# A macaron layer with 4-bit weights: order and engines of the unpacking in the first stage

## The chip, the core and the metric

The kernel runs on one core of a Trainium2 chip. Its time is that of the device, in microseconds (us); the number given is a median over runs. The profile's engines are TensorE (PE: matmuls; PEld: its weight loads), VectorE (DVE), ScalarE (ACT), GpSimd (POOL) and SyncE (SP), which mostly issues transfers (DMAs). A name with a q (SPq) is an engine's queue.

## The reference

Two half-weighted gated feed-forward blocks stand around a convolution, each behind a layer norm and added to its input. The feed-forward weights are 4-bit numbers, eight to an int32 word, with a zero point and a scale for each group of 128 input rows.

```python
def _dequant(qweight, scales, qzeros, g_idx):          # shifts = 4 * (0 .. 7)
    w = (qw[:, None, :] >> shifts[None, :, None] & MAXQ).reshape(-1, qweight.shape[1])
    z = ((qz[:, :, None] >> shifts[None, None, :] & MAXQ) + 1).reshape(qzeros.shape[0], -1)
    return (w.astype(scales.dtype) - z[g_idx].astype(scales.dtype)) * scales[g_idx]

def _L0_ffn_ref(x, ...):
    h = _silu(xf @ Wg) * (xf @ Wu)                     # HID 1024, INTER 2752, groups of 128 rows
    return (h @ Wd).reshape(...)

def _L0_attn_ref(u, ...):                              # S4: a long convolution along each row
    y = jnp.fft.irfft(jnp.fft.rfft(u, n=n) * jnp.fft.rfft(K, n=n), n=n)[..., :L]
    return y + D[0] * u

x = L0_attn_u                                          # (2, 1024, 1024) float32
x = x + 0.5 * _L0_ffn_ref(_layernorm(x), ...)
x = x + _L0_attn_ref(_layernorm(x), ...)
x = x + 0.5 * _L0_ffn_ref(_layernorm(x), ...)
```

## The kernel before, in words

**Jobs and steps.** The 2048 rows of x are taken in four batches of 512, each through two feed-forward blocks: eight jobs, with the convolution between two blocks hung beside the steps of other jobs. A job has a gate/up stage of 64 steps and a down stage of 44. The 43 units of 128 gate or up columns go in eight waves: five of six units, two of four, one of five (lines 38 and 39); a wave has eight steps, one for each group of 128 input rows. In a step each unit gets two matmuls, for the high part (xTh, rounded float32) and the low part (xTl, float16) of the input (line 689). Then ACT or DVE multiplies the unit's PSUM bank in place by a ratio of two groups' scales (lines 659 and 661); here this is called an eviction. The unit's next matmul waits for it. After a wave's last step g, hf, hh and hl are made (lines 714 to 724).

**Unpacking, once.** Only the first job unpacks. For each wave, words (fetch) and spread zero points (fetch_zeros) are loaded; DVE splits the words into two arrays of signed bytes in six operations (signed_bytes: two shifts with masks, two additions, two XORs); POOL copies out eight strided byte planes (dequantize), and each is stored by SP in a DRAM scratch, wq. Every job then loads byte tiles of 128 rows from wq four steps ahead of use (load_bytes, line 621) and POOL, or in the first job at some steps ACT, casts them to float32 three steps ahead (make_weights, lines 635 and 637). Waves 1 to 7 are unpacked beside the steps of the wave before, as first_weights lays down; the down weights follow in the same manner. POOL also makes hh and hl.

**Opening.** start runs ahead of step 0. Wave 0 is split by first_split; ACT makes the four even planes and POOL the four odd ones. Of each plane SP sends sixteen rows directly into the first byte tile (line 496) and the whole to wq (line 497). Meanwhile the moments of the first four row tiles are taken (ACT for tiles 1 and 3, DVE for 0 and 2), the rows are normalized (first_rows) and turned by PE transposes (first_turn), with a copy on ACT (xTh) and a subtraction on DVE (xTl) for each of eight chunks. Chunks 0 and 1 are in start, 2 to 7 at steps 0 to 5, chunk g is used from step g on. keep_warm issues transposes without use on PE. zero_points makes the table of zero points in DRAM, from which fetch_zeros reads; scales turns scale rows into the ratios.

**What sets the order.** at(up, s, f) hangs f on step s; it is written before that step's matmuls. The framework then orders each engine's instructions by its own reckoning, except where in_order_of_writing chains those of named engines. Each engine, and SP with its DMA queue, goes through its list in order and stops at the first entry that must wait. Buffers come from rings: ten of 4 KB a partition (t4: x, words, zeros, even, long scale rows), four for byte planes (qpool), six byte tiles, five weight tiles.

In before, a wave's schedule is this, with s0 = 8w - 12 for w above 2:

```python
at(up, s0 - 3, lambda both=both: in_order_of_writing(both, ET.SP))   # word and zero loads
in_pieces(at, [(up, s0 - 1)], lambda w=w: split(w))                  # six DVE operations, one step
s = s0 + j if w > 2 else j // 2 + s0 * (w - 1)                       # eight copies and stores
```

Of the kernel before, what the change touches and what calls it, by code (L numbers as in the profile page):

```python
# [55 lines left out]
def macaron_s4_kernel(  # L56
# [250 lines left out]
    def zero_points(which, z):  # L307

        p, n = z.shape
        zi, tab = (t2(f"{a}_{which}").bitcast(I32)[:p, : 8 * n] for a in ("zi", "ztab"))  # L310
        unpacked_zeros(tab, z, zi)
        dst, seg, queue = (zd_dram, SEGD, nc.sync) if which else (z_dram, SEG, nc.scalar)
        queue.dma_start(dst.rearrange("g (s n) -> (g s) n", s=seg), tab)

    def inverse(inv, s, name):

# [5 lines left out]
    def scale_rows(k0, k1, queue=nc.sync):  # L322
        n = k1 - k0
        row = t4(f"srow_{k0}") if n > 4 else t2(f"srow_{k0}")
        for m, src in enumerate((gate_s, up_s)):
            queue.dma_start(row[m * GK : (m + 1) * GK, : n * P], src[:, k0 * P : k1 * P])
        return row

    def scales(k0, k1, row):


        n = k1 - k0
        ps = bank(f"ps_s{k0}")
        u0, u1 = 2 * k0, 2 * k1
        for k in range(n):
            nc.tensor.transpose(
                ps[:, bass.ts(k, 2 * GK)], row[: 2 * GK, bass.ts(k, P)], ident[: 2 * GK, : 2 * GK]
            )
        if k1 == WIDE:
            row = t2("srow_half")  # L340
            for m, src in enumerate((gate_s, up_s)):
                nc.sync.dma_start(row[:GK, m * HALF : (m + 1) * HALF], src[:, WIDE * P :])
            nc.tensor.transpose(ps[:, bass.ts(2 * n, GK)], row[:GK, :P], ident[:GK, :GK])
# [131 lines left out]
    def first_split(zq):  # L475


        n = width_of(0)
        z, zi, even = (t4(f"{a}_w0").bitcast(I32)[:, :n] for a in ("z", "zi", "even"))
        raw = packed.pop(0)[0]  # L480
        unpacked_zeros(z, zq, zi)
        nc.vector.tensor_scalar(even, raw, 3, NIBBLES, ALU.logical_shift_left, ALU.bitwise_and)
        nc.vector.tensor_scalar(raw, raw, 1, NIBBLES, ALU.logical_shift_right, ALU.bitwise_and)
        for part in (even, raw):
            both = part.bitcast(U16)
            nc.vector.tensor_tensor(both, both, z.bitcast(U16), ALU.add)
        nc.vector.tensor_scalar(both, both, 0x8080, None, ALU.bitwise_xor)

        def dequantize(j):
            q = qpool.tile([P, n], I8, tag="q", name=f"q_0_{j}")  # L490
            view = lambda a, dt: a.bitcast(dt).rearrange("p (n k) -> p k n", k=4)[:, j // 2, :]
            if j % 2:
                nc.gpsimd.tensor_copy(q, view(raw, I8))
            else:
                nc.scalar.activation(q, view(even, U8), AF.Identity, bias=minus_128)
            nc.sync.dma_start(first_tile[j:P:8], q[: P // 8])
            nc.sync.dma_start(w_q[0].rearrange("(r j) n -> j r n", j=8)[j], q)

        return dequantize

    def signed_bytes(key, raw, even, z):

        nc.vector.tensor_scalar(even, raw, 3, NIBBLES, ALU.logical_shift_left, ALU.bitwise_and)
        yield
        nc.vector.tensor_scalar(raw, raw, 1, NIBBLES, ALU.logical_shift_right, ALU.bitwise_and)
        yield
        for part in (even, raw):
            both = part.bitcast(U16)  # L510
            nc.vector.tensor_tensor(both, both, z.bitcast(U16), ALU.add)  # L511
            yield
            nc.vector.tensor_scalar(both, both, 0x8080, None, ALU.bitwise_xor)
            yield
        view = lambda a: a.bitcast(I8).rearrange("p (n k) -> p k n", k=4)
        packed[key] = view(even), view(raw)

    def split(w):
        raw, z = packed[w]
# [59 lines left out]
    def first_weights(up, dn, at):  # L579


        for w in range(1, len(WAVES)):
            s0 = 8 * w - 12 if w != 2 else 7
            if w > 1:
                both = lambda w=w: (fetch(w), fetch_zeros(w))
                at(up, s0 - 3, lambda both=both: in_order_of_writing(both, ET.SP))
                in_pieces(at, [(up, s0 - 1)], lambda w=w: split(w))
            else:
                both = lambda: [None for _ in split(1)]
                at(up, 0, lambda both=both: in_order_of_writing(both, *STARTING))  # L590
            for j in range(8):
                s = s0 + j if w > 2 else j // 2 + s0 * (w - 1)
                at(up, s, lambda w=w, j=j: dequantize(w, j))
        s0 = len(STEPS) - 12
        when = lambda n: (up, s0 + n) if n < 12 else (dn, (5 * (n - 12)) // 6)
        for n in range(6 * 8):
            k, j = divmod(n, 8)
            a, rt = divmod(k, 3)
            if j == 0:
                at(*when(max(0, n - 7)), lambda a=a, rt=rt: fetch_down(a, rt))  # L600
                steps = [when(max(0, n - d)) for d in (4, 3, 3, 2, 1, 0)]
                in_pieces(at, steps, lambda a=a, rt=rt: split_down(a, rt))
            at(*when(n), lambda a=a, rt=rt, j=j: dequantize_down(a, rt, j))
# [743 lines left out]
    def fast():  # L1347
        for j, (b, k) in enumerate(JOBS):
# [49 lines left out]
                    at(up, 4, store)  # L1398
            if j == 0:
                rows = {3: srow_next}  # L1400
                for s, k0, k1 in ((4, 3, 9), (16, 9, 15), (32, 15, WIDE)):
                    if k0 > 3:
                        load = lambda k0=k0, k1=k1: rows.update({k0: scale_rows(k0, k1)})
                        at(up, s - 5, load)
                    at(up, s - 2, lambda k0=k0, k1=k1: scales(k0, k1, rows.pop(k0)))
                at(up, 40, scales_down)
                zeros = lambda: zero_points(1, zeros_down)
                at(up, 12, lambda: in_order_of_writing(zeros, ET.DVE, ET.SP))
                for c in range(2, NC):
# [46 lines left out]
    STARTING = ET.Activation, ET.DVE, ET.SP  # L1456
    first = {}

    def first_moments():
# [32 lines left out]
    def first_turn(c):  # L1492
# [20 lines left out]
    def keep_warm(n, src=None):  # L1513
# [5 lines left out]
    def start():  # L1519
# [32 lines left out]
        return rows_next, zeros_down  # L1552

    srow_next, zeros_down = in_order_of_writing(start, *STARTING, ET.PE)
# [88 lines left out]
```

## Time and profile before

| | |
|---|---|
| median of 3 runs | 2140.01 us (2137.66 to 2141.07) |
| profiled execution: its time, its span | 2140.35 us, 2138.6 us |
| first gate/up matmul | 21.75 us |
| end of the first job's gate/up stage | about 204 us |
| first gate/up matmul of the second job | about 300 us |
| PE busy in 0 to 20, 20 to 40, 60 to 80 us | 6.07, 15.26, 15.94 us |
| PE busy in 100 to 160 us | 60.00 us |
| granted PE clock over the whole span | 0.995 |

Times within the profile count from the span's start. A matmul's end is modelled, so PE can be shown busy without being at its peak; the number of matmuls in a window says more. Engines other than PE may idle without cost as long as PE is fed.

### The profile page before, as it was taken

The numbers are of one execution on the slowest core, as the hardware profiler recorded it, in microseconds if no ns is written. First come the engines' busy times: TensorE is split into PE (matmuls) and PEld (weight loads), VectorE is DVE, ScalarE is ACT, GpSimd is POOL, SyncE is SP. The second block draws the span as 40 slices with busy tenths as digits, with TensorE's granted clock in tenths as the row PEclk, the third lists the DMA queues.
The fourth block names the chain that finished last, engine by engine and source line by source line (L and its number), as shares of the span: only waits on it lengthen the run. The fifth ranks groups of instructions, "written<-read, shape, count | busy, mean of one in ns | idle before, by whom it ended". The sixth has DMA issues, their size and how long they took to land.

```text
span 2138.6 us, 30244 instructions
## 1 busy us (share of the span) xinstructions
PE 2089.9 (98%) x9744; PEld 1426.0 (67%) x9744; DVE 1700.3 (80%) x2785; ACT 1420.2 (66%) x2233; POOL 1055.2 (49%) x1424
## 2 busy tenths in 40 slices
PE   6899999999999999999999999999999999999998
PEld 4455675677776578665876568675686766866576
DVE  8888877779888777778777888878788787777776
ACT  6787777746655776676766766547776467767765
POOL 3767848653354543546335543454534545345642
PEclk9999999999999999999999999999999999999999
DMA  4335322112111211212121121112111121121111
GB/s 140 108 87 149 91 81 55 35 55 78 43 38 54 91 51 44 74 32 93 54 81 38 30 72 38 36 52 78 35 37 38 52 97 45 45 81 35 33 35 58
DMA packets 163686, 132.14 MB, mean 62 GB/s; under 512 B 22651, under 2 KB 151172, under 8 KB 163518
## 3 DMA queue, kind: packets, MB, share of 16 engines
q1 hardware_dynamic: 162646, 128.65, 19.8%
q8 instruction: 79, 1.29, 0.3%
q10 hardware_dynamic: 872, 1.47, 0.2%
q14 instruction: 89, 0.73, 0.1%
HBM read 104.45 MB, written 25.50 MB: 61 GB/s over the span
## 4 chain that ended last, share of the span: by engine, by line
PE 89%; DVE 6%; POOL 2%; DMA 1%; issue 1%; ACT 1%; SPq 0%; ACTq 0%; DVEq 0%; POOLq 0%
PE pg L689 54%; PE po L752 27%; PE pc L1078 3%; PE pb L774 1%; DVE pg L661 1%; PE pb L1078 1%; PE pt L228 1%; DVE po L661 1%; PE st L228 1%; DMA wq<-q 0%; DMA z<-z_dram 0%; DVE hf L719 0%; DVE hf_half L733 0%; DVE rawd L511 0%; POOL w_down L637 0%
## 5 line engine op out<-in xcount | busy, mean ns | idle before, releaser
L659 ACT ACTIVATE pg<-pg,rat 128x512 f32<-128x512 f32 x1240 | 786.1, 660 | 426.5 <-PE pg L689 425.5
L661 DVE TENSOR_TENSOR pg<-pg,rat 128x512 f32<-128x512 f32 x1168 | 777.2, 693 | 174.9 <-PE pg L689 170.3
L689 PE MATMUL pg<-xTh,w_up 128*128 128x512 f32 x2752 | 857.8, 439 | 5.2 <-DVE pg L661 4.1
L689 PE MATMUL pg<-xTl,w_up 128*128 128x512 f16 x2752 | 724.0, 383 | 3.2 <-DVE pg L661 1.4
L689 PEld LDWEIGHTS pg<-xTh,w_up 128*128 128x128 f32 x2752 | 520.3, 189 | 180.3 <-DVE pg L661 17.6
L637 POOL CAST w_up<-b 128x768 fp32r<-128x768 int8 (+2 forms) x490 | 375.2, 771 | 535.5 <-PE pg L689 421.6
L752 PE MATMUL po<-hl,w_down 128*128 128x512 f32 x1344 | 539.3, 403 | 8.5 <-DVE po L661 7.0
L659 ACT ACTIVATE po<-po,ratd 128x512 f32<-128x512 f32 x660 | 430.9, 661 | 159.4 <-PE po L752 159.0
L752 PE MATMUL po<-hh,w_down 128*128 128x512 f32 x1344 | 523.0, 392 | 0.0
L661 DVE TENSOR_TENSOR po<-po,ratd 128x512 f32<-128x512 f32 x620 | 427.0, 697 | 97.3 <-PE po L752 93.1
L689 PEld LDWEIGHTS <-w_up 128*128 128x128 bf16 x2752 | 228.3, 99 | 328.6 <-issue 155.9
L637 POOL CAST w_down<-bd 128x512 fp32r<-128x512 int8 x352 | 221.5, 631 | 411.3 <-PE po L752 341.1
L752 PEld LDWEIGHTS po<-hl,w_down 128*128 128x128 f32 x1344 | 252.0, 188 | 85.9 <-DVE po L661 19.8
L752 PEld LDWEIGHTS po<-hh,w_down 128*128 128x128 f32 x1344 | 252.8, 188 | 45.6
L723 POOL TENSOR_TENSOR hl<-hf,hh 128x512 fp32r<-128x512 f32 x168 | 216.8, 1290 | 7.7
L719 DVE SCALAR_TENSOR_TENSOR hf<-pg,rat,g 128x512 f32<-128x512 f32 x168 | 122.9, 747 | 44.9 <-ACT g L716 37.8
L716 ACT ACTIVATE g<-pg,rat 128x512 f32<-128x512 f32 x168 | 110.7, 686 | 49.4 <-PE pg L689 39.6
L721 POOL CAST hh<-hf 128x512 fp32r<-128x512 f32 x168 | 105.9, 630 | 56.0 <-PE pg L689 32.3
L187 DVE BATCH_NORM_STATS2 stats<-x 128x6 f32<-128x512 f32 x88 | 58.5, 676 | 0.5
L1108 DVE TENSOR_TENSOR x<-x,pc 128x512 f32<-128x512 f32 x32 | 21.9, 685 | 36.9 <-PE pc L1078 36.9
L1078 PEld LDWEIGHTS pc<-near,st 128*128 128x128 f32 x256 | 43.6, 191 | 7.9
L776 DVE TENSOR_TENSOR x<-x,pb 128x512 f32<-128x512 f32 x64 | 43.1, 678 | 6.2 <-PE pb L774 6.2
(205 smaller groups left out, 1034.8 us busy)
## 6 DMA issues: line engine op xcount, KB each, us to landing
b<-wq SPq DMA_DIRECT2D x319, 96.0 KB
bd<-wdq SPq DMA_DIRECT2D x336, 64.0 KB
x<-in_L_attn_u_dram SPq DMA_DIRECT2D x30, 512.0 KB
b<-wq SPq DMA_DIRECT2D x128, 64.0 KB
xs<-x SPq DMA_DIRECT2D x16, 512.0 KB
x<-xs SPq DMA_DIRECT2D x16, 512.0 KB
out_dram<-x SPq DMA_DIRECT2D x16, 512.0 KB
b<-wq SPq DMA_DIRECT2D x64, 80.0 KB
```

The costliest lines, as they stand in the source:

```text
L187: nc.vector.bn_stats(stats[:, t, i, :], x[b][t][:, bass.ts(i, 512)])
L637: nc.gpsimd.tensor_copy(t, b)
L659: nc.scalar.activation(dst, src, AF.Copy, scale=sc)
L661: nc.vector.tensor_tensor(dst, src, sc.to_broadcast([P, TB]), ALU.mult)
L689: nc.tensor.matmul(p, weights, (lo, hi)[k][:, g, :], start=(g == 0 and not done), stop=(g == GK - 1 and done), skip_group_check=True,)
L716: nc.scalar.activation(g, pg, AF.Silu, scale=rat[:, 2 * f, GK - 1 :])
L719: nc.vector.scalar_tensor_tensor(hf, pu, last, g, ALU.mult, ALU.mult)
L721: nc.gpsimd.tensor_copy(hi, hf)
L723: nc.gpsimd.tensor_tensor(lo, hf, hi.bitcast(F32), ALU.subtract)
L752: nc.tensor.matmul(ps[c], w[:, bass.ts(c, P)], part, start=(f == 0 and k == 0), stop=(f == NF - 1), skip_group_check=True,)
L776: nc.vector.tensor_tensor(part, part, ps, ALU.add)
L1078: nc.tensor.matmul(dst, lhsT, rhs, start=start, stop=stop, skip_group_check=True)
```

## The change

It concerns the first job alone, but for one order of operations that the down weights share.

- Loads: words and zeros of wave 2 are loaded in start; those of wave w + 1 are hung on step s0 + 3 of wave w, where s0 is now 8w - 15 (0 and 3 for waves 1 and 2). Scale rows are loaded at steps 6 and 11 for use at 14 and 30, in a chained order on SP.
- Split: one of its six operations a step (wave 1: in steps 0 to 3), with the even half finished before the odd half begins. The copies follow, even planes first; a wave's last is at s0 + 8.
- Opening: POOL makes six of wave 0's planes and ACT two. The stores of POOL's six to wq are issued by POOL. The even array gets one more XOR on DVE, on the upper half of each word. The planes' buffers come from another ring.
- The table of zero points is made right after the first 128 columns are normalized, and its store is issued by SP instead of ACT.
- The second half of all rows is normalized by ACT. Chunks 5 to 7 are copied by ACT into a buffer, and POOL makes both parts from it. keep_warm makes 22 transposes instead of 18.

```diff
@@ zero_points @@
-        dst, seg, queue = (zd_dram, SEGD, nc.sync) if which else (z_dram, SEG, nc.scalar)
-        queue.dma_start(dst.rearrange("g (s n) -> (g s) n", s=seg), tab)
+        dst, seg = (zd_dram, SEGD) if which else (z_dram, SEG)
+        nc.sync.dma_start(dst.rearrange("g (s n) -> (g s) n", s=seg), tab)
@@ first_split @@
+        def rest():
+            upper = even.bitcast(U16).rearrange("p (n k) -> p n k", k=2)[:, :, 1]
+            nc.vector.tensor_scalar(upper, upper, 0x8080, None, ALU.bitwise_xor)
+
         def dequantize(j):
-            q = qpool.tile([P, n], I8, tag="q", name=f"q_0_{j}")
+            q = t2(f"q_0_{j}").bitcast(I8)[:, :n]
             view = lambda a, dt: a.bitcast(dt).rearrange("p (n k) -> p k n", k=4)[:, j // 2, :]
-            if j % 2:
-                nc.gpsimd.tensor_copy(q, view(raw, I8))
+            if j in (0, 2):
+                nc.scalar.activation(q, view(even, U8), AF.Identity, bias=minus_128)
             else:
-                nc.scalar.activation(q, view(even, U8), AF.Identity, bias=minus_128)
+                nc.gpsimd.tensor_copy(q, view(raw if j % 2 else even, I8))
             nc.sync.dma_start(first_tile[j:P:8], q[: P // 8])
-            nc.sync.dma_start(w_q[0].rearrange("(r j) n -> j r n", j=8)[j], q)
+            queue = nc.sync if j in (0, 2) else nc.gpsimd
+            queue.dma_start(w_q[0].rearrange("(r j) n -> j r n", j=8)[j], q)
@@ signed_bytes @@
-        nc.vector.tensor_scalar(even, raw, 3, NIBBLES, ALU.logical_shift_left, ALU.bitwise_and)
-        yield
-        nc.vector.tensor_scalar(raw, raw, 1, NIBBLES, ALU.logical_shift_right, ALU.bitwise_and)
-        yield
-        for part in (even, raw):
+        for part, (n, shift) in zip((even, raw), shifts):
             both = part.bitcast(U16)
+            nc.vector.tensor_scalar(part, raw, n, NIBBLES, shift, ALU.bitwise_and)
+            yield
             nc.vector.tensor_tensor(both, both, z.bitcast(U16), ALU.add)
             yield
             nc.vector.tensor_scalar(both, both, 0x8080, None, ALU.bitwise_xor)
             yield
@@ first_weights @@
         for w in range(1, len(WAVES)):
-            s0 = 8 * w - 12 if w != 2 else 7
-            if w > 1:
-                both = lambda w=w: (fetch(w), fetch_zeros(w))
-                at(up, s0 - 3, lambda both=both: in_order_of_writing(both, ET.SP))
-                in_pieces(at, [(up, s0 - 1)], lambda w=w: split(w))
-            else:
-                both = lambda: [None for _ in split(1)]
-                at(up, 0, lambda both=both: in_order_of_writing(both, *STARTING))
-            for j in range(8):
-                s = s0 + j if w > 2 else j // 2 + s0 * (w - 1)
-                at(up, s, lambda w=w, j=j: dequantize(w, j))
+            s0 = (0, 3, 8 * w - 15)[min(w, 3) - 1]
+            steps = (0, 1, 2, 2, 3, 3) if w == 1 else range(6)
+            in_pieces(at, [(up, s0 + d) for d in steps], lambda w=w: split(w))
+            copies = {1: (2, 2, 3, 3, 3, 3, 3, 3), 2: (3, 3, 4, 4, 6, 6, 7, 7)}
+            if 1 < w < len(WAVES) - 1:
+                both = lambda w=w: (fetch(w + 1), fetch_zeros(w + 1))
+                at(up, s0 + 3, lambda both=both: in_order_of_writing(both, ET.SP))
+            for k, d in zip((0, 2, 4, 6, 1, 3, 5, 7), copies.get(w, (3, 3, 4, 5, 6, 6, 7, 8))):
+                at(up, s0 + d, lambda w=w, k=k: dequantize(w, k))
@@ fast, first job @@
-                for s, k0, k1 in ((4, 3, 9), (16, 9, 15), (32, 15, WIDE)):
+                for first_use, s, k0, k1 in ((5, 0, 3, 9), (14, 6, 9, 15), (30, 11, 15, WIDE)):
                     if k0 > 3:
                         load = lambda k0=k0, k1=k1: rows.update({k0: scale_rows(k0, k1)})
-                        at(up, s - 5, load)
-                    at(up, s - 2, lambda k0=k0, k1=k1: scales(k0, k1, rows.pop(k0)))
+                        at(up, s, lambda load=load: in_order_of_writing(load, ET.SP))
+                    at(up, first_use, lambda k0=k0, k1=k1: scales(k0, k1, rows.pop(k0)))
@@ first_moments, inside the loop over row tiles 0 and 2 @@
+            between[t]()
@@ first_rows @@
-        if t % 2:
+        if t % 2 or half:
@@ first_turn @@
-        nc.scalar.copy(hi, ps)
-        nc.vector.tensor_tensor(lo, ps, hi.bitcast(F32), ALU.subtract)
+        if c < 5:
+            nc.scalar.copy(hi, ps)
+            nc.vector.tensor_tensor(lo, ps, hi.bitcast(F32), ALU.subtract)
+        else:
+            both = gpool.tile([P, TB], F32, tag="g", name=f"turn_0_1_{c}")
+            nc.scalar.copy(both, ps)
+            nc.gpsimd.tensor_copy(hi, both)
+            nc.gpsimd.tensor_tensor(lo, both, hi.bitcast(F32), ALU.subtract)
@@ rows_by_chunk @@
-            for t in (2 * c - 4, 2 * c - 3):
-                first_rows(t, 512, HID)
+            first_rows(2 * c - 4, 512, HID)
@@ start @@
-        dequantize_first = first_split(zq)
-        mv, scratch = first_moments()
-        for j in (1, 3, 5, 7, 0, 2, 4, 6):
+        rest, dequantize_first = first_split(zq)
+        for j in (1, 3, 5, 7):
+            dequantize_first(j)
+        mv, scratch = first_moments({0: rest, 2: lambda: None})
+        for j in (4, 6, 0, 2):
             dequantize_first(j)
...
-        keep_warm(18, scratch)
+        keep_warm(22, scratch)
...
         for t in range(NT):
             first_rows(t, 0, P)
+        zero_points(0, zeros)
+        for t in (0, 2):
+            first_rows(t, P, 512)
         first_turn(0)
+        for t in (1, 3):
+            first_rows(t, P, 512)
         keep_warm(6)
-        for t in range(NT):
-            first_rows(t, P, 512)
         scales(0, 3, srow)
         first_turn(1)
-        zero_points(0, zeros)
+        for t in (1, 3):
+            first_rows(t, 512, HID)
         fetch_zeros(1)
+        fetch(2)
+        fetch_zeros(2)
```

More of the change, by code (lines that the diff above doesn't have):

```diff
@@ L326, in scale_rows, with scales @@
             queue.dma_start(row[m * GK : (m + 1) * GK, : n * P], src[:, k0 * P : k1 * P])
-        return row
-    def scales(k0, k1, row):
+        if k1 < WIDE:
+            return row, None
+        half = t2("srow_half")
+        for m, src in enumerate((gate_s, up_s)):
+            queue.dma_start(half[:GK, m * HALF : (m + 1) * HALF], src[:, WIDE * P :])
+        return row, half
+    def scales(k0, k1, rows):
         n = k1 - k0
+        row, half = rows
         ps = bank(f"ps_s{k0}")
@@ L339, in scales @@
         if k1 == WIDE:
[L340 to L343, printed above, removed]
+            nc.tensor.transpose(ps[:, bass.ts(2 * n, GK)], half[:GK, :P], ident[:GK, :GK])
             u1 = UNITS
@@ L487, in first_split @@
         nc.vector.tensor_scalar(both, both, 0x8080, None, ALU.bitwise_xor)
+        def rest():
+            upper = even.bitcast(U16).rearrange("p (n k) -> p n k", k=2)[:, :, 1]
+            nc.vector.tensor_scalar(upper, upper, 0x8080, None, ALU.bitwise_xor)
         def dequantize(j):
-            q = qpool.tile([P, n], I8, tag="q", name=f"q_0_{j}")
+            q = t2(f"q_0_{j}").bitcast(I8)[:, :n]
             view = lambda a, dt: a.bitcast(dt).rearrange("p (n k) -> p k n", k=4)[:, j // 2, :]
-            if j % 2:
-                nc.gpsimd.tensor_copy(q, view(raw, I8))
+            if j in (0, 2):
+                nc.scalar.activation(q, view(even, U8), AF.Identity, bias=minus_128)
             else:
-                nc.scalar.activation(q, view(even, U8), AF.Identity, bias=minus_128)
+                nc.gpsimd.tensor_copy(q, view(raw if j % 2 else even, I8))
             nc.sync.dma_start(first_tile[j:P:8], q[: P // 8])
-            nc.sync.dma_start(w_q[0].rearrange("(r j) n -> j r n", j=8)[j], q)
-        return dequantize
+            queue = nc.sync if j in (0, 2) else nc.gpsimd
+            queue.dma_start(w_q[0].rearrange("(r j) n -> j r n", j=8)[j], q)
+        return rest, dequantize
     def signed_bytes(key, raw, even, z):
-        nc.vector.tensor_scalar(even, raw, 3, NIBBLES, ALU.logical_shift_left, ALU.bitwise_and)
-        yield
-        nc.vector.tensor_scalar(raw, raw, 1, NIBBLES, ALU.logical_shift_right, ALU.bitwise_and)
-        yield
-        for part in (even, raw):
+        view = lambda a: a.bitcast(I8).rearrange("p (n k) -> p k n", k=4)
+        packed[key] = view(even), view(raw)
+        shifts = (3, ALU.logical_shift_left), (1, ALU.logical_shift_right)
+        for part, (n, shift) in zip((even, raw), shifts):
             both = part.bitcast(U16)
+            nc.vector.tensor_scalar(part, raw, n, NIBBLES, shift, ALU.bitwise_and)
+            yield
             nc.vector.tensor_tensor(both, both, z.bitcast(U16), ALU.add)
@@ L514, in signed_bytes @@
             yield
-        view = lambda a: a.bitcast(I8).rearrange("p (n k) -> p k n", k=4)
-        packed[key] = view(even), view(raw)
     def split(w):
@@ L1457, in macaron_s4_kernel, with first_moments @@
     first = {}
-    def first_moments():
+    def first_moments(between):
         stats = small.tile([P, NT, 2, 6], F32, tag="stats", name="stats_0_1")
```

## The prediction

> **What bounds the kernel now.** I read the page first, part 4: it says whose work ends last.
>
> ```profile
> PE 89%; DVE 6%; POOL 2%; DMA 1%; issue 1%; ACT 1%; SPq 0%; ACTq 0%; DVEq 0%; POOLq 0%
> ```
>
> TensorE (PE) sets the time over the whole span. The change touches only the first of eight jobs, so what counts there is the time in which PE is not fed. Next come the windows of 5 us, with the columns PE, PEld, DVE, ACT and POOL busy, then granted clock, DMA share and GB/s.
>
> ```profile
> 35.00:40.00 5.00, 2.79 (x16) 1.87 (x15) 5.00 (x10) 2.92 (x5) 5.00 (x7) 0.93 0.17 59
> 40.00:45.00 5.00, 5.00 (x20) 2.71 (x20) 4.58 (x8) 2.76 (x5) 2.34 (x4) 0.73 0.29 98
> ...
> 60.00:65.00 5.00, 5.00 (x23) 2.85 (x23) 3.89 (x7) 3.63 (x6) 5.00 (x7) 1.00 0.06 20
> ...
> 70.00:75.00 5.00, 1.71 (x10) 1.24 (x9) 3.13 (x8) 1.82 (x4) 0.09 (x1) 0.84 0.41 123
> 75.00:80.00 5.00, 4.23 (x10) 1.55 (x11) 3.79 (x7) 1.41 (x2) 5.00 (x6) 0.50 0.55 158
> ...
> 175.00:180.00 5.00, 3.50 (x15) 1.57 (x13) 4.97 (x7) 2.31 (x4) 3.52 (x5) 1.00 0.82 248
> ```
>
> A fed PE starts some 90 gate/up matmuls in 20 us, 0.222 us each, so 688 of them take 153 us. The first job's run from 21.6 to 204, 183 us. About 4 us of the 30 over are transposes that stay; **some 26 us are loss**, the most that the stage could give back. Counting matmuls against 0.222 us places it: about 6 us in steps 0 to 7 (to 52), 6.5 from 70 to 80, 1 at 95 to 97, over 4 from 175 to 204. In 35 to 40 DVE has no free moment. The hole at 70 is read in the chain of waits:
>
> ```profile
> 64.78 0.78 POOL q L544
> ...
> 65.57 0.32 SPq L545
> ...
> 65.94 1.23 SPq L454
> ...
> 68.40 4.61 DMA z<-z_dram
> ...
> 73.03 0.96 DVE even L511
> ...
> 75.66 0.62 DVE pg L661
> ...
> 76.32 5.79 PE pg L689 x16
> ```
>
> SP stands at a store (L545) until POOL has made its bytes, only then issues the word loads (L454) and zero loads behind it; 4.61 us later DVE, which had the addition at the head of its queue, goes on, and only then evicts the banks that PE waits for.
>
> **The change part by part.** All times are made against the profiled run (2140.35 us, span 2138.6).
>
> Opening, to the first gate/up matmul (21.75 now). ACT loses two casts (919 ns each), but the normalization behind them waits for the bias (16.42), so it starts 0.47 earlier, no more. Four more warm transposes (18 took 4.07, so 0.9) end the warming at 18.6 and shift the first turn to about 19.6; its copy ends near 20.2. DVE now makes the zero table (eight of 1.51 together, one of 1.05) ahead of the first rows: 16.94 + 2.56 + 1.4 = 20.9, then the first low half 0.68, 21.6: **no gain, no loss**. The extra XOR (some 0.56, as L487) lies in DVE's waits before 13.47. The scale chain behind is 0.5 later, but 2.5 us of table work are gone from behind it, where DVE has no free time.
>
> On SP, eight first-tile rows and eight stores (0.50 and 0.58 each) become eight rows and two stores. Six stores go to POOL: no POOL-issued DMA stands in the trace, so this cost is unknown. From 8.81 POOL has six copies of 0.78, six issues of c, then the first weight cast (0.83, now begun at 20.16). At c = 1.0 that cast begins at 19.5. The next chunk's load waits for the six stores: 13.5 + 6c, about 2 to land (L497's took 1.84), 2.4 for the load (21.32 to 23.70 now): 23.9 against 23.70. Its weights are needed about 25.7, so **up to c = 1.2 it costs nothing**; each further 0.1 costs 0.6. [...] The row is the four POOL copies from 8.81: 3.13 together, unstretched, beside DVE's moments. [...]
>
> ```profile
> 34.37 1.43 POOL L544 COPY q<-even 128x768 int8<-128x768 int8 x1 [3.99 <-DVE even L513]
> ...
> 36.84 0.84 POOL L544 COPY q<-raw 128x768 int8<-128x768 int8 x1
> ```
>
> The first ran into DVE's L511 at 34.16 and lost 0.6. In the opening DVE runs moments, tiny operations and one XOR, so I take c = 1.0[...].
>
> Steps 0 to 7. DVE's work from 16.94 to the last evictions of step 7, from rows: now eight low halves (5.2), normalization 2.9, scales 3.6, table 2.5, split of wave 1 4.0, evictions 19 × 0.62 = 11.8, and 2.9 of wave 2's split: 33 us, ending near 50, with its waits 52, as seen. Taken away: three low halves (2.0) and two normalizations of 512 (1.5); wave 2's share grows by 0.3 and the interference falls: about 29.5, so near 48. ACT gains two normalizations (0.81 each) ahead of the first evictions, which begin near 25.2 instead of 22.82; step 1 then ends near 28.5, as now, because DVE's evictions (now held until 26.59) come early. POOL gets three casts and three subtractions (0.56 and 1.28, 5.5 us) beside eight copies: reckoned in its new order, with the weight of step 7 free to cast when step 2 is done, it ends the last low half near 46, four wave-2 copies follow, and step 8's weights come near 50. The later of the two counts: 50 against 52.5. DVE alone would give 4.1 and POOL 2; I take **-3.0** (0 to -6).
>
> [...] PE's hole of 2.21 us before 38.36 was followed by a clock of 0.82 in 38 to 40, 0.50 in 40 to 42 and 0.89 in 42 to 45, which is another 1.7 lost. [...] I follow the row: the -3.0 may be taken whole although the sum of pure waits is smaller.
>
> Waves 2 to 7. The word and zero loads move from two steps ahead of the split to six; a step is 2.67 us, loads land within 7. The new SP order has wave 3's loads (now behind the store at 64.78) straight after the third byte load of wave 1, near 46, and its split at 53. Later waves' loads stand behind byte loads with one to two steps left. Scale rows for step 14 are loaded eight steps ahead, which ends PE's own wait for them (3.29 at 74.04). Gone are the hole and the slow clock after it: 70 to 80 made some 13 matmuls, 2.9 us, and 0.5 of transposes: **-6.5**. The eight zero operations for the down stage stay at step 12 (3.1 us on DVE), now between evictions; without the hole they may cost 0.5 of it.
>
> One split operation a step (0.5 to 1.1) instead of 3.9 in one: the idle 0.91 at 95 to 100 goes, **-0.9**. The copies now end at step 8w-7 instead of 8w-5. For the last wave that matters: POOL waits 3.09 there for stores that lie behind the 512 KB rows of x (5.47 to land, at 164.20), and the bytes reach PE at 180.66. In the new order four of its stores precede all x loads and all copies are earlier: the idle 2.07 of 175 to 185 goes, taken as **-1.5**. DVE's split of the down weights at 186 to 189 stays in one step, and so does its loss.
>
> Sum: -3.0 - 6.5 - 0.9 - 1.5 = -11.9: 2128.4 for the profiled run, 2128 as a median (the runs shown lie 0.3 lower). The jobs after it start earlier and are otherwise as before.
>
> **Rivals.** (1) *POOL becomes the bound in steps 3 to 8*: 5.5 us more in front of casts. For it, POOL's full windows at 35 to 45; against, its idle 3.75 and 5.23 before the casts at 46.09 and 52.15. Steps 0 to 7 then give +2 with a slow clock: 2133. (2) *A load is late again at wave 4 or 6*, whose loads reuse buffers of scale rows that PE must first have read. One hole like the one at 70 stays: 2135. (3) *Everything works*: steps 0 to 7 reach PE's own pace (-6), the tail gives 3: about 2122. (4) *Slower*: the six POOL stores. The price is 6c - 7.2 on the first chunk of bytes; it eats the gain at c = 3.2, and is slower beyond the resolution from c = 3.9; at c = 4.5, 2148. Against it, DVE's light work there. (5) *The loads are issued earlier but land no earlier*, because SP still stops at other stores: SP waits 43.5 us for POOL's copies over the stage, but the order shows the loads past them. It gives 2135 to 2138.
>
> **How the numbers follow.** Forecast 0.58; rival 1 0.12; 2 0.09; 3 0.11; 4 0.05; 5 0.05. A measurement of this kernel tells 0.2% (4.3 us) from no change, so faster means below 2135.7: forecast, 1, 3 and most of 2, 0.87; slower 0.05; the rest 0.08. The forecast's own ends (steps 0 to 7 from 0 to -6, the hole from -4 to -7, the rest from 0 to -4.5) are 2122 to 2136; with the rivals 2118 to 2138.
>
> **What would show it.** Right: no DVE wait for z near 70; no window of the first job below 0.9 clock after 30; the first gate/up matmul within 0.5 of 21.75; step 8 near 50; the second job 12 us earlier, with later jobs as long as now. Wrong: POOL idle or issuing between 13 and 20 with the second cast after 25.5; PE waiting for POOL's low halves at steps 5 to 7; a DVE wait for z at a later wave; a PE wait for bytes near 168.

## The result and the profile after

| | before | changed |
|---|---|---|
| median | 2139.82 us (2136.34 to 2144.43, 18 runs) | 2134.94 us (2132.28 to 2139.55, 18 runs) |
| ratio to before, 95% interval | | 0.9979 (0.9972 to 0.9986) |
| profiled execution, its span | 2140.35, 2138.6 us | 2136.97, 2135.1 us |

The gain is 4.9 us by the medians and 3.5 by the two profiled spans; 11.9 was forecast. To see where it came from, the first job is cut by PE's own work, at the starts of its 688 gate/up matmuls; a wave of six units has 96 of them. The tile view shows 96 up to 53.15 us in before, then 96 up to 55.40 us in the changed kernel (count, duration min/median/max in ns, first and last start):

```profile
L689 PE MATMUL pg<-xTl,w_up x48: 377/379/650, 21.7 to 52.5; 128*128 128x512 f16 x48
L689 PE MATMUL pg<-xTh,w_up x48: 387/486/988, 22.2 to 53.0; 128*128 128x512 f32 x48
```

```profile
L695 PE MATMUL pg<-xTl,w_up x49: 376/379/650, 22.0 to 55.2; 128*128 128x512 f16 x49
L695 PE MATMUL pg<-xTh,w_up x47: 387/398/988, 22.5 to 54.8; 128*128 128x512 f32 x47
```

Counted so for all waves, in us (a stretch ends where PE starts the first matmul after its share; a few of them may belong to the next wave already):

| stretch | before | changed | difference | forecast |
|---|---|---|---|---|
| to the first gate/up matmul | 21.75 | 22.04 | +0.3 | 0 |
| the first 96 matmuls (steps 0 to 7) | 31.4 | 33.4 | +2.0 | -3.0 |
| wave 1 (the hole at 70 to 80) | 30.3 | 24.7 | -5.7 | -6.5 |
| wave 2 (idle at 95 to 100) | 22.9 | 21.7 | -1.2 | -0.9 |
| waves 3 to 5 | 60.0 | 60.4 | +0.4 | 0 |
| waves 6 and 7 (tail) | 36.9 | 35.9 | -1.0 | -1.5 |
| from the last of them to the second job's first | 96.0 | 97.1 | +1.1 | 0 |
| the rest of the span | 1839.1 | 1839.8 | +0.7 | 0 |

The recorded expectations of the runs below use another mark for a wave's end, the start of DVE's first hf behind it: 55.3 and 84.3 for waves 0 and 1 in before, 55.0 and 79.5 in the changed kernel. By that mark steps 0 to 7 seem 0.5 us shorter, but PE had by then started 102 matmuls in before and only 95 in the changed kernel. For the same 96 it needed 2.0 us more.

On the page, PE still carries the chain, and the row of the low matmuls (count, then busy time and mean ns, then idle time before them and what ended most of it) names a releaser that it did not name before:

```profile
PE 88%; DVE 6%; POOL 2%; DMA 1%; issue 1%; ACT 1%; SPq 0%; ACTq 0%; DVEq 0%; POOLq 0%
...
L695 PE MATMUL pg<-xTl,w_up 128*128 128x512 f16 x2752 | 722.0, 382 | 8.5 <-POOL xTl L1518 3.2
```

The row's idle time was 3.2 us before, the largest share of it (1.4) ended by DVE's evictions. The windows of the changed kernel, columns as before (PE, PEld, DVE, ACT, POOL, clock, DMA share, GB/s):

```profile
35.00:40.00 5.00, 4.49 (x26) 2.74 (x26) 5.00 (x7) 4.52 (x9) 4.86 (x5) 1.00 0.12 39
40.00:45.00 5.00, 4.20 (x19) 2.08 (x18) 5.00 (x10) 2.75 (x5) 5.00 (x6) 1.00 0.18 62
45.00:50.00 5.00, 2.12 (x6) 1.52 (x6) 5.00 (x8) 0.60 (x1) 4.92 (x6) 0.83 0.28 84
50.00:55.00 5.00, 4.65 (x18) 2.01 (x16) 3.12 (x5) 3.63 (x7) 4.03 (x5) 0.83 0.64 180
...
70.00:75.00 5.00, 4.11 (x22) 2.08 (x20) 5.00 (x11) 3.36 (x7) 4.87 (x5) 1.00 0.51 145
75.00:80.00 5.00, 5.00 (x24) 2.85 (x23) 5.00 (x13) 3.97 (x8) 1.60 (x2) 1.00 0.86 253
```

The hole at 70 to 80 is gone, as said: 40 gate/up matmuls there instead of 14 (the rows' 46 and 20 count six transposes each). But a new one stands at 45 to 50, with six matmuls. The timeline has PE's idle time in brackets, and windows of 2 us behind it show the clock:

```profile
47.88 1.05 PE L695 MATMUL pg<-xTl,w_up 128*128 128x512 f16 x3 [3.16 <-POOL xTl L1518]
```

```profile
48.00:50.00 2.00, 2.00 (x6) 1.42 (x5) 2.00 (x3) 0.60 (x1) 1.92 (x3) 0.58 0.29 72
50.00:52.00 2.00, 2.00 (x7) 0.65 (x6) 0.87 (x2) 1.38 (x3) 2.00 (x3) 0.57 0.50 123
```

PE waits 3.16 us, and the slow clock costs about 1.7 more (an estimate from these two rows: 0.42 and 0.43 of 2 us each). The chain of waits of the changed kernel shows what POOL was doing (start, duration, what):

```profile
46.60 1.23 POOL xTl L1518
47.83 0.55 POOL xTh L1517
...
48.47 1.38 POOL xTl L1518
...
53.25 0.79 POOL w_up L643
```

POOL is done with the low halves of chunks 6 and 7 at 47.83 and 49.85; PE needs them for steps 6 and 7. The forecast had POOL done near 46. Its first rival, POOL as the bound in steps 3 to 8, has happened: it named +2 for these steps with a slow clock.

A profile is one execution. Those below lay between 2.6 us under and 4.9 over the median of their own kernel. Seven kernels below that have the same program in steps 0 to 7 differ there by up to 1.1 us, so a stretch is read to about 1 us. Ratios are against runs of before on the same chip.

### The profile page after: what moved, and what is told of

Read it like the earlier page. It is cut to its first block, busy times and chain, and to the rows that moved or that the text cites. A ratio compares the mean times of both kernels' runs of the same rounds, so it can differ in the third digit from the quotient of the medians.

```text
span 2135.1 us, 30272 instructions
## 1 busy us (share of the span) xinstructions
PE 2087.0 (98%) x9748; PEld 1425.8 (67%) x9748; DVE 1702.1 (80%) x2781; ACT 1420.6 (67%) x2233; POOL 1072.9 (50%) x1438
## 4 chain that ended last, share of the span: by engine, by line
PE 88%; DVE 6%; POOL 2%; DMA 1%; issue 1%; ACT 1%; SPq 0%; ACTq 0%; DVEq 0%; POOLq 0%
PE pg L695 53%; PE po L758 27%; PE pc L1084 3%; DVE pg L667 2%; PE pb L780 1%; PE pb L1084 1%; PE pt L228 1%; DVE po L667 1%; PE st L228 1%; DVE hf L725 1%; POOL q L551 0%; POOL qd L580 0%; POOL xTl L248 0%; DMA b<-wq 0%; POOL w_down L643 0%
## 5 line engine op out<-in xcount | busy, mean ns | idle before, releaser
L643 POOL CAST w_up<-b 128x768 fp32r<-128x768 int8 (+2 forms) x490 | 377.4, 776 | 519.0 <-PE pg L695 407.9
L643 POOL CAST w_down<-bd 128x512 fp32r<-128x512 int8 x352 | 222.4, 634 | 410.2 <-PE po L758 338.6
L1114 DVE TENSOR_TENSOR x<-x,pc 128x512 f32<-128x512 f32 x32 | 22.0, 686 | 36.9 <-PE pc L1084 36.9
```

What stands on the lines that cost most here:

```text
L643: nc.gpsimd.tensor_copy(t, b)
```

## Experiments

Each kernel is the changed one with the edit shown, unless said.

**Chunks 5 to 7 off POOL.**

```diff
-        if c < 5:
+        if c < 8:
```

> The changed kernel with chunks 5 to 7 again copied by ACT and subtracted by DVE, as before; POOL loses three casts and three subtractions (some 5.9 us as they ran), DVE gets three subtractions (2.0 us). Theory A (POOL is the bound from 33 to 54 us): the first weights of step 8 are cast some 2.5 us earlier, the end of wave 0 comes near 53 and that of wave 1 near 77.5 instead of 79.5; 2 us faster than the changed kernel, near 2133. Theory B (DVE is the bound there and POOL only stood beside it): wave 0 ends at 55 to 57, wave 1 at 80 to 81.5, no gain or up to 1.5 us lost, near 2136.

Measured: 2134.13 us, ratio 0.9973 (0.9965 to 0.9982). By DVE's mark wave 0 ends at 52.1 and wave 1 at 76.3. PE starts its first 96 matmuls in 28.2 us, 5.3 less than in the changed kernel and 3.3 less than in before. Its windows:

```profile
40.00:45.00 5.00, 5.00 (x24) 2.68 (x23) 5.00 (x10) 4.10 (x8) 3.75 (x4) 1.00 0.29 98
45.00:50.00 5.00, 4.31 (x17) 2.10 (x16) 5.00 (x12) 3.13 (x6) 3.36 (x4) 1.00 0.47 127
```

PE is fed and the clock stays at 1.00: theory A. DVE's three subtractions cost nothing visible in these steps; wave 1 then takes 26.5 us instead of 24.7. Every later profile agrees: the eight kernels with these chunks off POOL need 27.7 to 29.2 us for the first 96 matmuls, the eight with them on POOL (the changed one among them) 32.0 to 36.8. But of the 2.7 us that were ahead at the end of wave 5, 0.1 were left at the end of wave 7, and by its times this kernel cannot be told from the changed one.

**Step 8's weights ahead of four copies.** The chain shows w_up L643 last before step 8; one edge puts that cast ahead of the copies.

```diff
+        if w == 2:
...
+            tc.add_manual_dep(copy, cast_8[0].name, no_sync, reason="order of writing")
```

> The changed kernel with one edge more: on POOL the cast of step 8's weights stands ahead of the four even copies of wave 2, which stood ahead of it and took 3.47 us. Theory A (these copies are what delays step 8): the cast starts near 51.2, when its bytes land, instead of 53.20, step 8 near 52, and wave 1 ends 2 us earlier, near 77.5; time near 2133. Theory B (from 54 us on DVE, not POOL, sets the pace of wave 1): step 8 starts earlier but wave 1 still ends at 79 to 79.5, and the time stays near 2135.

Measured: 2137.0 us, 0.9981 (0.9974 to 0.9988): no gain. The cast began at 51.49, 1.7 us earlier, yet wave 0 ended at 56.9 by DVE's mark, in an execution that was 1.1 us late by 45 already, and the first 96 matmuls took 33.8 us. The chain names what came last, not by how much: in the changed kernel PE had waited 0.35 us for this cast and 3.16 for the low half of chunk 6, and that wait was still 3.14 here.

**Wave 2's loads out of the opening.** `fetch(2)` and `fetch_zeros(2)` go from start to step 1, in a chained order on SP.

> The changed kernel with the loads of wave 2's words and zeros moved from the opening to step 1. They stand ahead of the bytes of step 5, which were issued at 27.53 and landed at 32.6; ACT's cast of these bytes stands ahead of its copies of chunks 5 to 7, for which POOL waits. Theory (POOL's late start, after 6 us of idle before 33.04, makes wave 0 late): the bytes land near 29 to 30, POOL's first low half ends 2 us earlier, wave 0 ends near 53 and wave 1 near 77.5; time 2133. Rival (POOL is bound by DVE's split of wave 1, not by ACT): wave 0 ends at 54.5 to 55.5 and nothing is gained; or the words of wave 2 are now late and wave 1 ends later than 79.5.

Measured: 2138.95 us, 0.9987 (0.9978 to 0.9995), rather a loss. The first 96 matmuls took 32.0 us, 1.4 less than in the changed kernel, but wave 1 took 27.4, 2.7 more (81.1 by DVE's mark, as the rival said). ACT cast the bytes of step 5 at 30.11 instead of 32.68, but the loads now stood ahead of step 6's bytes, whose cast began at 33.24, and POOL ended its last low half at 49.44 instead of 49.85. POOL's work also ran slowly: in the changed kernel eight copies, three casts and three subtractions took from 35.14 to 49.85, 14.7 us, where durations from before (0.84, 0.56 and 1.28) make 12.2.

**All stores of wave 0 issued by SP.**

```diff
-            queue = nc.sync if j in (0, 2) else nc.gpsimd
+            queue = nc.sync
```

> The changed kernel with all eight stores of wave 0's planes issued by SP, as before (six were POOL's; 0.53 to 0.64 us of POOL each in its trace). If POOL's issuing is what holds up DVE's small shift (L198, 2.07 us at 13.84) then that shift falls below 1 us, and the first gate/up matmul comes near 21; otherwise it stays at 2 us and at 22.0. SP has 3.5 us more to issue, which puts the second byte load at 22 to 23 instead of 21.3 and may cost what was gained. Either way the end of wave 0 stays within 0.7 of 55.0 and the time within 2 us of the changed kernel's, 2135.

Measured: 2135.18 us, 0.9972 (0.9959 to 0.9985), no difference that can be told. In the opening the timelines show what POOL's stores did. First POOL and then DVE in the changed kernel, then DVE in this one (start, duration, operation):

```profile
13.21 1.07 POOL L505 DMA_DIRECT2D wq<-q  x2
14.28 1.59 POOL L502 COPY q<-even_w 128x768 int8<-128x768 int8 x2
```

```profile
13.84 2.07 DVE L198 TENSOR_SCALAR half<-ve 128x4 int32<-128x4 int32 x1
```

```profile
14.26 0.17 DVE L198 TENSOR_SCALAR half<-ve 128x4 int32<-128x4 int32 x1
```

A shift of four elements a partition stood for 1.9 us until POOL's two stores and two copies were done, in the middle of the chain that makes the bias (18.12 instead of 16.64). Without the stores the first gate/up matmul came at 21.4 instead of 22.0. The price came behind it: SP reached the second byte load at 22.05 instead of 21.32 and step 5's at 29.00 instead of 27.53, and these bytes landed at 35.29 instead of 32.61. In the chain of the changed kernel, then of this one:

```profile
27.53 5.08 DMA b<-wq
```

```profile
29.00 6.29 DMA b<-wq
```

ACT cast them 2.7 us later, POOL's work for chunks 5 to 7 and wave 1 began at 37.83 instead of 35.14, took 14.7 us again, and PE's first 96 matmuls took 36.8 us, 3.4 more. By DVE's mark wave 0 ended at 57.7, not within 0.7 of 55.0 as expected. This execution was 3.2 us over its kernel's median, so how much of that is usual stays open; the times of the two kernels do not differ.

**The loads alone.** Before, with only this:

```diff
-                at(up, s0 - 3, lambda both=both: in_order_of_writing(both, ET.SP))
+                at(up, s0 - 6, lambda both=both: in_order_of_writing(both, ET.SP))
-                        at(up, s - 5, load)
+                        at(up, s - 10, lambda load=load: in_order_of_writing(load, ET.SP))
```

> The kernel before with nothing changed but the loads: words and zeros of waves 2 to 7 are hung three steps earlier, the second and third scale rows five steps earlier and in a chained order on SP. If the loads are the whole gain: no DVE wait for zeros near 70, wave 1 ends near 80 instead of 84.3, and the time falls by 4 to 5 us, as with the whole change. If the packing of one operation a step is needed for it (loads issued earlier but the split still in one step, 3.9 us of DVE ahead of evictions): wave 1 ends at 82 to 84 and the gain is at most 2 us.

Measured: 2139.91 us, 0.9995 (0.9986 to 1.0004). DVE no longer waits for zeros near 70, but wave 1 still took 29.7 us (30.3 in before); the chain now ran over POOL's copies of wave 2, hung as late as before, their store, and the bytes behind it (20 gate/up matmuls from 70 to 80). Wave 2 took 21.8 instead of 22.9: PE ran it without a break, although the split was still in one step:

```profile
87.83 22.33 PE pg L689 x99
```

In waves 6 and 7 the run then lost 2.8 us (39.8); by what is not shown. For wave 1 the early loads alone are worth little; what the packing and the early copies are worth without them was not tried.

**The down stage's zeros, from step 12 to 40.**

```diff
-                at(up, 12, lambda: in_order_of_writing(zeros, ET.DVE, ET.SP))
+                at(up, 40, lambda: in_order_of_writing(zeros, ET.DVE, ET.SP))
```

> The changed kernel with the table of the down stage's zero points (eight operations on DVE, 3.0 us at 68.25, and one more) hung on step 40 instead of step 12. Theory B (DVE is the bound of wave 1, from 54 to 74): wave 1 ends 1.5 to 3 us earlier, near 77, and the time falls by as much. Theory A (wave 1 is only late because it starts late): wave 1 ends near 79.5 as now, and the time does not change.

Measured: 2138.39 us, 0.9990 (0.9983 to 0.9997), rather slower than the changed kernel, with wave 1 at 27.5 us (26.2 by DVE's mark): both theories failed. Its chain shows why:

```profile
73.38 0.83 POOL q L551
74.21 0.08 SPq L552
...
74.34 4.03 DMA b<-wq
```

Wave 2's first bytes took 4.03 us to land. On SP the word and zero loads of wave 4 (issued at 71.22 to 73.32) now stood just ahead of them; with the table at step 12 they come after (73.48). So in a further run they were held back as well:

```diff
-                at(up, s0 + 3, lambda both=both: in_order_of_writing(both, ET.SP))
+                at(up, s0 + (6 if w == 3 else 3), lambda both=both: in_order_of_writing(both, ET.SP))
```

> The changed kernel with the down stage's zero table on step 40, as in the run that made wave 1 longer (26.1 us), and in addition the word and zero loads of wave 4 hung on step 15 instead of 12. If these loads are what made the first bytes of wave 2 late there: the bytes land in 2 to 2.5 us, the hole at 75 to 80 (2.30 busy of 5, clock 0.72 behind it) goes, wave 1 takes 22 to 23 us and the time is near 2132.5. If POOL's copies of wave 2's planes are late anyway: wave 1 takes 25 or more, the time stays near 2138.

Measured: 2135.37 us, 0.9973 (0.9962 to 0.9984), 3.0 us under the run without this edit; wave 1 took 24.5 us (23.8 by DVE's mark), and the same bytes:

```profile
74.73 2.10 DMA b<-wq
```

PE's idle time there fell from 2.70 to 0.34 us. A load hung early delayed bytes that were wanted sooner (4.03 us to land against 2.10). Against the changed kernel, though, moving the table and these loads gave next to nothing: waves 1 and 2 take 46.1 us together instead of 46.4.

**Two casts from POOL to ACT** (steps 11 and 12; `or s in (11, 12)` in make_weights).

> The changed kernel with the weights of steps 11 and 12 cast by ACT instead of POOL (1.65 us from POOL to ACT). Theory A (POOL, busy 14.9 of 15 us from 60 to 75, is what keeps wave 1 at 24.5 us): wave 1 takes 23 to 23.5, the second job starts 1 us earlier, near 294.3. Theory B (DVE, also without a free moment there, with the eight zero operations of 3.0 us, sets the pace): wave 1 takes 24.5 or more, since ACT can then take fewer evictions from DVE; time unchanged or up to 1 us more.

Measured: 2141.02 us, 1.0001 (0.9992 to 1.0009): wave 1 took 29.2 us (27.5 by DVE's mark). Relieving POOL alone made it worse: again the chain held a byte load that landed late (4.19 us, at 78.04) behind wave 4's loads (74.45 to 76.54). Whether that is the cause was not tried here.

**x behind the last wave's stores.** The four 512 KB loads are chained on SP where step 55 hangs them, so behind the bytes of step 59.

```diff
-                    at(up, 55 if j == 0 else 6, lambda: load_x(ab, rows_of(u, ab)))
+                    loads = lambda: load_x(ab, rows_of(u, ab))
+                    chained = lambda: in_order_of_writing(loads, ET.SP)
+                    at(up, *((55, chained) if j == 0 else (6, loads)))
```

> The changed kernel with the four 512 KB loads of x chained on SP behind the byte loads of step 59, so behind all stores of the last wave. Theory (the last store took 6.26 us to land because these loads stand ahead of it, and PE waits for the bytes behind it): the store lands in about 2 us, PE's loss in 170 to 175 (3.23 busy of 5) goes, and the end of the last wave comes 1.5 to 2 us earlier, near 196; the second job then starts near 293.5 and the time is near 2133. Rival: the rows of x come later into the down stage and the gain is given back there; the second job starts at 295 as now, time 2135.

The chain of the changed kernel at that place:

```profile
165.00 0.68 POOL q L551
...
165.69 6.26 DMA wq<-q
...
172.00 2.07 DMA b<-wq
```

Measured: 2134.38 us, 0.9964 (0.9951 to 0.9977). SP issued the first of those bytes at 167.99 instead of 172.00, PE ran through 170 to 175 without a gap, waves 6 and 7 took 34.7 instead of 35.9, and the second job began at 293.4, 1.9 us earlier; by the times the two kernels cannot be told apart. With x ahead of the stores these two waves took 34.6 to 39.8 us in the profiles, with x behind them 34.7 to 34.8 in seven of eight: that was where the run with the chunks alone lost its lead. Its PE stood there as long as in the changed kernel, 2.05 us, but behind it the clock fell, which cost some 1.3 us more (an estimate: 0.42 of 3 us). These 3 us in the changed kernel, where the clock stayed, and in the run with the chunks alone:

```profile
175.30:178.30 3.00, 3.00 (x14) 1.46 (x15) 1.40 (x2) 2.72 (x5) 2.15 (x4) 1.00 0.39 104
```

```profile
172.60:175.60 3.00, 2.98 (x9) 1.41 (x9) 0.70 (x1) 2.56 (x5) 2.20 (x4) 0.58 0.41 118
```

**Together.** First with wave 2's loads at step 1 too, then without, then with the two casts on ACT:

> The changed kernel with three edits together: chunks 5 to 7 on ACT and DVE again, wave 2's loads at step 1, the loads of x chained behind the last wave's stores. If they act on separate losses: wave 0 ends near 51 to 52, wave 1 near 75, the last wave near 193 to 194, the second job starts near 290, and the time is 2130 to 2131, faster than both kernels. If the gain of the first 80 us is lost again at the end as in the run with the chunks alone: the last wave near 197, time 2134.

> The changed kernel with two edits together: chunks 5 to 7 again on ACT and DVE, and the loads of x chained behind the last wave's stores. The first gave 2.9 us up to wave 5 and lost it in the last two waves, the second gave 1.9 us at the start of the second job. If the loss at the end is the late store behind x alone: wave 0 ends at 52, wave 1 at 76, wave 5 near 160.5, the last wave near 194 to 195, the second job starts near 291, time 2130 to 2131. If something else at the end is as late: the last wave near 197, time 2133 to 2134.

> The two edits (chunks 5 to 7 on ACT and DVE, loads of x behind the stores) and the casts of steps 11 and 12 on ACT. With chunks 5 to 7 off POOL, PE waited near 70 for bytes behind a plane that POOL copied at 66.34; if POOL's load is the cause, those copies come 1.6 us earlier, the hole at 65 to 71 (3.14 busy of 5) shrinks, wave 1 ends near 75 and the time is near 2129.5. If DVE is the cause: as the two edits alone, 2130.5 or more.

Measured: 2131.29 us, 0.9950 (0.9936 to 0.9963); 2133.86, 0.9965 (0.9952 to 0.9979); 2132.41, 0.9956 (0.9943 to 0.9970). The second job began at 293.5, 291.4 and 289.5. The first of the three was profiled in an execution of 2136.21 us, its others were 2130.44 to 2131.78; there the zero table ran into ten POOL operations in a row, PE stood 4.13 us behind it, and wave 1 took 31.1:

```profile
63.88 5.95 DVE L290 TENSOR_SCALAR zi<-zq 84x32 int32<-84x32 int32 x8
```

In the changed kernel the eight took 3.10 us. In the third, wave 1 took 26.1, in the second 26.8, so two casts off POOL brought next to nothing there either.

**The table and wave 4's loads in that company.** The third kernel with the table on step 20; the same with wave 4's loads on step 15; then these loads with the table back on step 12, and on step 40:

> As the run with the chunks, x and the two casts, and the table of the down stage's zero points on step 20 instead of 12, where PE keeps its pace and DVE has some 0.7 us of 5 free. If these nine operations (3 to 3.9 us on DVE, in one profile 5.9 beside POOL's copies) are what keeps wave 1 long: wave 1 takes 22 to 22.5 us, the second job starts near 289, time near 2128. If they only move their loss into wave 2: wave 2 takes 22.5 to 24 instead of 21.5 and the time is as without the move.

> The run with chunks 5 to 7 on ACT and DVE, x behind the stores, two casts on ACT and the zeros on step 20, and in addition wave 4's loads on step 15. If these loads made the hole at 70 to 75 (2.57 busy of 5): waves 1 and 2 take 23 and 21.5 instead of 24.5 and 24.8, the second job starts near 288.5, time 2128 to 2129. Otherwise as without the later load, 2135.9.

> The run with chunks 5 to 7 on ACT and DVE, x behind the stores and two casts on ACT (2132.4), and in addition wave 4's loads on step 15; the zeros stay on step 12. If the zeros' 3 us of DVE are what is left of wave 1's loss here: wave 1 takes 25 as without the later load and the time stays at 2131.5 to 2132.5. If the loads are: wave 1 near 23, time near 2130.

> Chunks 5 to 7 on ACT and DVE, x behind the stores, two casts on ACT, wave 4's loads on step 15, and the down stage's zeros on step 40. If the table is the loss: waves 1 and 2 take 22.4 and 21 (43.4 together, 47.7 with the table on step 20, 45.2 with it on step 12), wave 5, where the table then lies, at most 2 us longer; the second job starts near 288, time near 2129.5. If the loss belongs to DVE's and POOL's other work: 45 or more together, the second job at 290 or later, time 2131.5 or more.

| table on step | wave 4's loads on step | us | ratio | wave 1 | wave 2 | second job |
|---|---|---|---|---|---|---|
| 20 | 12 | 2135.86 | 0.9977 (0.9968 to 0.9986) | 27.9 | 24.0 | 292.9 |
| 20 | 15 | 2133.26 | 0.9962 (0.9948 to 0.9975) | 23.9 | 26.4 | 292.4 |
| 12 | 15 | 2131.74 | 0.9955 (0.9941 to 0.9969) | 26.1 | 21.7 | 289.2 |
| 40 | 15 | 2130.73 | 0.9957 (0.9943 to 0.9970) | 23.7 | 22.6 | 290.3 |

The third kernel itself had 26.1 and 21.7 too, so with the table on step 12 wave 4's loads made no difference here. With these loads on step 15, waves 1 and 2 together take 50.2 us with the table on step 20, 47.8 on step 12 and 46.3 on step 40, where wave 5 does not get longer by more than 0.4. In this company the table thus costs the two waves 1.5 us on step 12 and 3.9 on step 20. Of the 1.5, 1.1 are lost again in waves 6 and 7 (35.8); by what was not tried. The last two kernels and the first and third of those above cannot be told apart; all four lie below both kernels of the case, the ratio of the changed one being 0.9979.

## Why the prediction was wrong

The time fell, and 2134.94 lies in the range given, but the sum was 7 us too large, 8.4 in the profiles. Of these 8.4, 5.0 lie in one step, and there the direction was wrong too. By its own terms:

1. *Opening, 0.* Measured +0.3, as a sum of things not foreseen. What DVE lost to POOL's stores and copies (1.9 us on L198) was for the most part paid by the zero table, which ran in 0.83 + 0.52 instead of 1.51 + 1.05. The price of a POOL-issued store, taken as 1.0 us, was 0.54 (median of the six, 0.73 at most), and the fourth rival fell with it; from issue to landing the six took 1.9 us (median).
2. *Steps 0 to 7, -3.0: this step failed.* Measured +2.0. "DVE alone would give 4.1 and POOL 2; I take **-3.0**" set POOL's last low half near 46; it came at 49.85, PE stood 3.16 us for the one before it, and the clock fell. Two things make up the 3.9 us. POOL's work took 14.7 us instead of the 12.2 that rows of before give: the working priced it by an engine left alone, although the prediction itself showed a copy of 1.43 us beside DVE's split against 0.84, and eight of these copies were to run beside that very split. And it began only at 35.14, behind ACT's cast of step 5's bytes; even 12.2 from there end at 47.3. With chunks 5 to 7 off POOL the same 96 matmuls take 28.2 us, 3.3 less than in before, which is what the forecast had for this step. So the rest of the change delivered it, and moving these chunks to POOL turned it round. The first rival, given 0.12, is what came. By its own rule, that the later of two counts decides, the working had 2 to 2.5, not 3.0.
3. *The hole, -6.5.* Measured -5.7: the wait for zeros went and the slow clock with it, as described. The zero table, "without the hole they may cost 0.5 of it", does stand in the chain,

```profile
68.25 3.02 DVE zi L290 x8
71.26 0.59 DVE pg L667
```

   with DVE busy 24.96 of 25 us from 55 to 80, but away from it (and with wave 4's loads later) waves 1 and 2 are only 0.3 us shorter. What keeps wave 1 at 24.7 us, 3.4 over 96 matmuls at 0.222, is not shown. Nor were SP's late loads the whole cause: the loads alone gave 0.6 us of wave 1.
4. *Idle at 95 to 100, -0.9.* Measured -1.2, but not for the reason given, the split in single operations: the loads alone brought the same.
5. *Tail, -1.5.* Measured -1.0. The claim that "four of its stores precede all x loads" was right and not enough: the last store still stood behind x (6.26 us to land). With x behind the stores it is -2.2. That the clock stayed at 1.00 behind the gap of 2.05 us that was left was luck, as the run with the chunks alone shows (0.58 behind a gap of the same length).
6. *Later jobs, 0.* The down stage and the rest gave back 1.7 us. The profiles scatter there by more: from the last gate/up matmul to the second job 95.5 to 97.1 us, the changed kernel the most of all, and behind it 1837.9 to 1841.1. What makes this was not tried.

On the clock the prediction followed a row of before, and it held in the changed kernel: behind a gap of 3.16 us the clock was 0.58 and 0.57 in windows of 2 us. The third rival, with steps 0 to 7 at full pace, was not reached even by the best kernels, where the second job began 10 us earlier than before; its own terms make 2124, not 2122. The second and fifth, loads late again, did not occur in the changed kernel.

## What to carry to other kernels

Price work that is moved to an engine by rows of that engine beside the neighbour it will have, not by its quietest rows (here 14.7 us came instead of 12.2), and ask whether it stands in front of something that the bound engine needs soon. Compare stages at equal work of the bound engine, here at equal counts of matmuls: by a mark on another engine, between two of which PE started from 84 to 103, the stage that got 2.0 us slower looked 0.5 us faster. Where two engines and a queue are all nearly full, taking work from one may only show the next (with two casts off POOL wave 1 took 29.2 us instead of 24.7); undo pairs, and check what the freed queue now issues first.

## What the runs showed of the hardware

- Behind idle times of PE of 2.21 and 3.29 us in before and 3.16 us in the changed kernel the granted clock fell to 0.50 (windows of 1 us at 40 to 42, 75 to 80 and 49 to 51). Of two gaps of 2.05 us, shown above, one was followed by 0.58 over 3 us, the other by 1.00; behind 1.50 us in before, at 178.69, it stayed at 1.00. So at 2.05 us the length of a gap did not settle what it cost.
- A tiny DVE operation stood while GpSimd worked: a 128x4 shift that took 0.17 us in before stood 2.07 in the changed kernel, past two copies. Eight operations of 84x32 took 5.95 us beside ten GpSimd operations in the first of the three kernels with edits together, and 3.10 in the changed kernel.
- A store issued by GpSimd cost it 0.54 us (median of six, 0.73 at most), about SP's 0.58, while DVE took moments and ran 128x4 operations.
- An 80 KB store took 6.26 us to land with three 512 KB loads issued ahead of it, 5.47 in before with one; 96 KB of bytes behind another wave's words took 4.03 us, and 2.10 without these ahead of them.
